# Start of a fused AdaLN, Mamba and mixture-of-experts kernel: order of the first loads, and products that keep TensorE occupied

## The chip, the cores and the metric

The kernel runs on one core of a Trainium2 chip. Its time is the device time of one execution in microseconds (us). An execution that the hardware profiler took is shown beside it; its span is counted from the first to the last instruction of the program. The engines are named as in the profile: PE is TensorE (matmuls; PEld are its weight loads), DVE is VectorE, ACT is ScalarE, POOL is GpSimd, and SP is SyncE, whose queue issues nearly all DMAs.

## The reference

There are 8 sequences of 2048 tokens with 256 features, all in fp32. A conditioning row per sequence gives six modulation vectors. The input is normalized and modulated, goes through a Mamba-2 mixer with a gated residual, is normalized and modulated again, and goes through a dense mixture of 8 experts with a second gated residual.

```python
mod = (_silu(c) @ wmod).reshape(8, 6, 1, -1)
sa, ca, ga, sb, cb, gb = (mod[:, n] for n in range(6))
ga, gb = ((2 * (g >= 0) - 1) * maximum(abs(g), 0.25) for g in (ga, gb))
h = _layernorm(x) * (1 + ca) + sa
# mixer: h @ W_in gives z, xBC, dt; a causal depthwise convolution of 4 taps and silu on xBC;
# a scan over chunks with decay exp(cumsum(dt * A)); times silu(z); RMS norm; @ W_out
x = x + ga * mixer(h)
h = _layernorm(x) * (1 + cb) + sb
# experts: softmax gate, weights under 0.1 set to zero, the rest normalized
x = x + gb * sum(weight[:, e] * (h @ expert_w[e] + expert_b[e]) for e in range(8))
```

## The kernel before

The tokens are cut into 32 blocks of 512 (4 blocks a sequence), and each block into 4 chunks of 128 for the scan. Each block passes through stages: `fetch` (its rows, `xt`), `first_norm`, `project_xbc` with the convolution behind it, `project_z`, `silu_xbc`, `spread` and `within` for each chunk, `outputs`, `output` with `residual`, `gate_weights`, `experts`. A stage is a generator. `at(time, stage)` puts it into a heap of planned times, `run()` resumes the stage that is due first, and `yield d` lets it sleep for d planned microseconds. Blocks start 70 planned us apart, and so several are in work at once. The plan is only made when the program is written down, and the framework's scheduler can still move instructions: what the chip sees is one fixed order on each engine, which waits in order for its operands by semaphores. PSUM's 8 banks are handed out by `take` and `give`; a bank counts as free `READ_TIME` after it was given back.

These are the parts at the start, with their lines in the profile of before:

- Loads before the stages: on SP's queue the first half of `wmod` (into `ht1`, line L109, in the profile `ht<-in_L_wmod_dram`), the rows of block 0 (`load(0, 0)`, L105), the part of `w_in` for `xbc`, `dt` and the rest (L109), convolution weights (L143, L144), the part for `z`, the small vectors (`d_ch` L152, `dt_bias` and `a_log` L148), `norm_sb` (L156), `wo_n` (L157), two pieces `wgate` and the second half of `wmod` (L109), and gate weights. ACT's queue loads the conditioning (L114), and ACT takes its silu (L115).
- `condition`: two transposes of the conditioning on PE (L252), copies to `ct` by DVE (L253), then `modulation(0)`: 8 products of 8 columns (L262; an fp32 product is two instructions in the trace) and two reads by DVE into `mod_pp` (L267).
- `first_norm` and `modulated`: statistics by DVE (L315, L316), `rstd` by POOL (L310, L311), `shift` by DVE (L324), `xn` by ACT (L328), transposes by PE (L338), and `ht` by ACT, which reads `mod_pp` (L340).
- `project_xbc`: 6 pairs of products (L409). Each bank is read by ACT (L364, and `halo` L368) and by three convolution taps on DVE (L372). `steps_of_time` stands beside it: `dt` products (L459), a softplus by Exp (L475) and Ln (L479) on ACT with steps on DVE between them (`sp_u` L481), and the running sum `cs` (L487). SP writes `cs` to DRAM (`cs_d`, L492), and `spread` reads it back to all partitions (`wide`, L512, 0.5 MB a chunk).
- `head_weights`: POOL copies `w_dt` (L177), and ACT takes the exponential of `a_log` (L178), for which it loads a table. `output_weights`: POOL scales `wo_n` (L276). `batch_gates`: products with `wgate` (L288).
- `expert_weights`: 4 loads of `eb_sb` (L168) and 8 of `we_sb` (L170), 0.25 MB each. In the order on SP's queue `cs_d` of block 0 stands behind the first `we_sb`, then come four more, `wide` of chunk 0, the last three, the rows of block 1, `wide` of chunk 1, and the rows of blocks 2 to 4.
- `within`: `w` and `wide` on ACT (L527, L541, L542), `xdt`, `sm` and `bm` on DVE (L545, L549, L551), `xdec` and `cw` on POOL (L558, L565), transposes and products on PE (L537 to L540, L576).

Of the kernel before, what the change touches and what calls it, by code (L numbers as in the profile page):

```python
# [15 lines left out]
P = 128  # L16
# [9 lines left out]
def kernel(  # L26
# [26 lines left out]
    nc = tc.nc  # L53
    B, L, DM = x.shape
# [10 lines left out]
    NC = T // P  # L65
    NSB = L // T
# [6 lines left out]
    def new(pool, shape, tag, bufs=None):  # L73
        n_names[0] += 1
        kw = {} if bufs is None else {"bufs": bufs}
        return pool.tile(shape, F32, tag=tag, name=f"{tag}_{n_names[0]}", **kw)
# [9 lines left out]
    upper = new(const, [P, P], "upper")  # L86
    make_upper_triangular(nc, upper, val=1.0, diag=True)
    ones = new(const, [P, P], "ones")
# [4 lines left out]
    io = ctx.enter_context(tc.tile_pool(name="io", bufs=5))  # L93
# [4 lines left out]
    sml = ctx.enter_context(tc.tile_pool(name="small", bufs=2))  # L98
    dram = ctx.enter_context(tc.tile_pool(name="dram", bufs=2, space=bass.MemoryType.DRAM))

    def load(b, s):
        xt = new(io, [P, NC, DM], "xt")
        nc.sync.dma_start(out=xt, in_=x[b, ts(s, T), :].rearrange("(c p) d -> p c d", p=P))  # L105
        return xt

    def columns(dst, src, first, count):
        nc.sync.dma_start(  # L109
            out=dst, in_=src[:, first : first + count].rearrange("(k p) n -> p k n", p=P)  # L110
        )
# [24 lines left out]
    nc.gpsimd.memset(w_dt, 0.0)  # L136
    a_pos = new(const, [P, 1], "a_pos")

    columns(wpp[0], wmod, 0, 2 * DM)
    first_x = load(0, 0)  # L140
    columns(w_in_sb[:, :, DI:], w_in, DI, NPROJ - DI)
    with nc.allow_non_contiguous_dma(reason="small vectors, an element or a few per partition"):
        nc.sync.dma_start(out=conv_w_sb, in_=conv_w.rearrange("(m p) k -> p m k", p=P))  # L143
        nc.sync.dma_start(out=conv_b_sb, in_=conv_b.rearrange("(m p) -> p m", p=P))  # L144
        columns(w_in_sb[:, :, :DI], w_in, 0, DI)
        for name, v in (("dt_bias", dt_bias), ("a_log", a_log)):
            for c in range(NC):
                nc.sync.dma_start(  # L148
                    out=heads[name][c * QD : c * QD + NH, :], in_=v.unsqueeze(1)
                )  # L150
        for q in range(2):
            nc.sync.dma_start(  # L152
                out=d_ch[ts(q, HEADDIM), :],
                in_=d_skip.rearrange("(m q) -> q m", q=2)[q].partition_broadcast(HEADDIM),
            )
        nc.sync.dma_start(out=norm_sb, in_=norm_w.rearrange("(m p) -> p m", p=P))  # L156
        nc.sync.dma_start(out=wo_n, in_=w_out.rearrange("(m p) o -> p m o", p=P))  # L157
        for g, part in enumerate((2, 5)):
            columns(wgate[:, :, g, :], wmod, part * DM, DM)
        columns(wpp[1], wmod, 3 * DM, 2 * DM)  # L160
        nc.sync.dma_start(
            out=gate_w_sb[:, :, :NE], in_=gate_w.rearrange("(k p) e -> p k e", p=P)
        )
    nc.sync.dma_start(out=heads["gate_b"], in_=gate_b.partition_broadcast(P))

    def expert_weights():
        for c in range(NC):
            nc.sync.dma_start(out=eb_sb[c * QD : c * QD + NE, c, :], in_=expert_b)  # L168
        for e in range(NE):
            nc.sync.dma_start(  # L170
                out=we_sb[:, :, e, :], in_=expert_w[e].rearrange("(k p) o -> p k o", p=P)
            )
            yield 2.0

    def head_weights():

        nc.gpsimd.tensor_copy(w_dt[:, :, :NH], w_in_sb[:, :, DI + CD : NPROJ])  # L177
        nc.scalar.activation(a_pos, heads["a_log"], AF.Exp)  # L178
        yield
# [6 lines left out]
    def at(time, stage):  # L186
        heapq.heappush(events, (time, n_events[0], stage))
        n_events[0] += 1
# [16 lines left out]
    def take(use, count=1):  # L205
        while True:
            now = clock[0]
            idle = sorted((t, i) for i, t in enumerate(free_at) if t <= now)
            held = sum(h == use and t > now for h, t in zip(holder, free_at))
            if len(idle) >= count and held + count <= MOST[use]:  # L210
                break
            yield 0.2
        got = []
        for _, i in idle[:count]:
            free_at[i], holder[i] = 1e9, use
            got.append(new(psum, [P, 512], f"bank{i}"))
            bank_of[got[-1].tensor.name] = i
        return got[0] if count == 1 else got

    def give(ps):  # L220
        free_at[bank_of.pop(ps.tensor.name)] = clock[0] + READ_TIME

# [2 lines left out]
        while any(step not in d for step in steps):  # L225
            yield 0.2

    order = [(b, s) for b in range(B) for s in range(NSB)]
    info = [{} for _ in order]
    gated, carry = {}, {}  # L230

# [7 lines left out]
        return t.unsqueeze(2).to_broadcast([P, NC, NE])  # L239

    def fetch(n):
        info[n]["x"] = first_x if n == 0 else load(*order[n])
        yield


# [1 line left out]
    ct = new(const, [P, KD, B], "ct")  # L247

    def condition():
        for k in range(KD):  # L250
            ps = yield from take("m")
            nc.tensor.transpose(ps[:, :B], cond_sb[:, ts(k, P)], ident[:B, :B])  # L252
            nc.vector.tensor_copy(ct[:, k, :], ps[:, :B])  # L253
            give(ps)
        yield from modulation(0)

    def modulation(half):
        ps = yield from take("m")
        for n in range(2):
            for d in range(KD):  # L260
                for k in range(KD):
                    nc.tensor.matmul(  # L262
                        ps[:, ts(n * KD + d, B)], wpp[half][:, k, n * DM + d * P :][:, :P],
                        ct[:, k, :], start=(k == 0), stop=(k == KD - 1),
                    )
        for n in range(2):
            nc.vector.tensor_scalar(  # L267
                mod_pp[:, 2 * half + n], ps[:, ts(n, KD * B)].rearrange("p (d b) -> p d b", b=B),
                float(n), None, ALU.add,
            )  # L270
        give(ps)

    def output_weights():

        for m in range(MI):
            nc.gpsimd.tensor_scalar(  # L276
                wo_n[:, m, :], wo_n[:, m, :], norm_sb[:, m : m + 1], None, ALU.mult
            )
        yield
# [475 lines left out]
    def experts(n):  # L755
# [32 lines left out]


    READ_TIME = 4.5  # L790
    PERIOD, XBC_STEP, Z_STEP, OUT_STEP = 70.0, 6.0, 3.5, 4.4
    STARTS = (
        (fetch, -20.0), (first_norm, -9.0), (project_xbc, 11.5), (project_z, 42.0),
        (silu_xbc, 47.5), (output, 128.0), (gate_weights, 156.0), (experts, 198.0),
    )
    at(-30.0, condition())
    at(12.0, head_weights())
    at(35.0, expert_weights())
    at(20.0, output_weights())
    at(30.0, modulation(1))  # L800
    for n in range(len(order)):
        start = n * PERIOD
# [41 lines left out]
```

## Time and profile before

| What | Before |
|---|---|
| median of 3 runs | 2406.21 us (2404.78 to 2408.36) |
| profiled execution, own time | 2408.26 us |
| its span | 2406.5 us |
| mean granted PE clock over the span | 0.988 |
| busy PE, DVE, ACT, POOL | 2327.3, 1830.3, 1621.4, 1128.7 us |
| HBM read, written | 89.47 MB, 18.87 MB |

The profile's page gives busy time by engine over the whole span. For the start, the answers by stretch give each engine's busy time, the granted PE clock and the DMA engines' share in a few microseconds, and the timeline gives every instruction with its start, its duration, and the idle time before it with what ended that. A wait counts only if the waiting engine, or one that waits for it, is late afterwards.

### The profile page before, as it was taken

The numbers are of one execution on the slowest core, as the hardware profiler recorded it, in microseconds if no ns is written. First come the engines' busy times: TensorE is split into PE (matmuls) and PEld (weight loads), VectorE is DVE, ScalarE is ACT, GpSimd is POOL, SyncE is SP. The second block draws the span as 40 slices with busy tenths as digits, with TensorE's granted clock in tenths as the row PEclk, the third lists the DMA queues.
The fourth block names the chain that finished last, engine by engine and source line by source line (L and its number), as shares of the span: only waits on it lengthen the run. The fifth ranks groups of instructions, "written<-read, shape, count | busy, mean of one in ns | idle before, by whom it ended". The sixth has DMA issues, their size and how long they took to land.

```text
span 2406.5 us, 33568 instructions
## 1 busy us (share of the span) xinstructions
PE 2327.3 (97%) x11602; PEld 1313.9 (55%) x11602; DVE 1830.3 (76%) x4414; ACT 1621.4 (67%) x2947; POOL 1128.7 (47%) x1244
## 2 busy tenths in 40 slices
PE   6889999999999999999999999999999999999998
PEld 3545555555555555555555555555555555555564
DVE  4777877777777787777887778777777787778775
ACT  6877676676666766667867667767677667667720
POOL 2554454443554435545445545445545445545442
PEclk8999999999999999999999999999999999999999
DMA  5111011110111101111111111111111111111100
GB/s 164 45 37 39 34 55 45 44 46 28 54 46 44 45 28 54 46 45 54 37 37 54 46 46 53 37 37 55 54 36 54 37 37 54 46 44 45 37 18 18
DMA packets 64601, 110.51 MB, mean 46 GB/s; under 512 B 7048, under 2 KB 47024, under 8 KB 64432
## 3 DMA queue, kind: packets, MB, share of 16 engines
q1 hardware_dynamic: 64416, 108.35, 13.3%
q8 instruction: 93, 1.52, 0.3%
q14 instruction: 76, 0.62, 0.1%
q10 hardware_dynamic: 16, 0.01, 0.0%
HBM read 89.47 MB, written 18.87 MB: 45 GB/s over the span
## 4 chain that ended last, share of the span: by engine, by line
PE 61%; ACT 11%; DVE 7%; POOL 6%; issue 1%; POOLq 0%; ACTq 0%
PE bank L781 26%; PE bank L662 8%; PE bank L409 7%; PE bank L445 6%; PE bank L608 4%; PE bank L576 3%; ACT w L527 3%; DVE xbc L372 2%; POOL cw L565 2%; PE bank L338 1%; PE bank L537 1%; ACT xn L328 1%; POOL rstd L311 1%; ACT wide L541 1%; DVE res L738 1%
## 5 line engine op out<-in xcount | busy, mean ns | idle before, releaser
L781 PE MATMUL bank<-we_sb,ht 128*128 128x512 f32 x2048 | 968.7, 598 | 18.3 <-DVE bm L551 15.6
L738 DVE SCALAR_TENSOR_TENSOR res<-bank,wt,res 128x256 f32<-128x256 f32 x1024 | 487.3, 476 | 212.6 <-PE bank L781 116.5
L781 PEld LDWEIGHTS bank<-we_sb,ht 128*128 128x128 f32 x2048 | 375.5, 191 | 398.8 <-issue 351.8
L372 DVE SCALAR_TENSOR_TENSOR xbc<-bank,conv_w_sb,xbc 128x511 f32<-128x511 f32 (+2 forms) x576 | 425.4, 740 | 96.0 <-ACT halo L368 94.9
L565 POOL TENSOR_TENSOR cw<-wide,xbc 128x1024 f32<-128x1024 f32 x128 | 305.7, 2388 | 274.5 <-ACT wide L541 157.2
L527 ACT ACTIVATE w<-wide,tok_major 128x128 f32<-128x128 f32 x1024 | 327.2, 390 | 137.8 <-PE bank L608 96.2
L409 PE MATMUL bank<-ht,w_in_sb 128*128 128x512 f32 x768 | 375.1, 611 | 5.6 <-DVE xbc L372 4.5
L445 PE MATMUL bank<-ht,w_in_sb 128*128 128x512 f32 x512 | 244.6, 601 | 1.0 <-ACT zs L432 1.0
L662 PE MATMUL bank<-wo,zs 128*128 128x256 f32 x1024 | 244.0, 380 | 0.3
L579 POOL TENSOR_TENSOR state<-state,wide 128x512 f32<-128x512 f32 x112 | 120.8, 1079 | 247.1 <-DVE state L590 216.7
L409 PEld LDWEIGHTS bank<-ht,w_in_sb 128*128 128x128 f32 x768 | 141.9, 194 | 163.6 <-issue 142.1
L340 ACT ACTIVATE ht<-bank,mod_pp 128x512 f32<-128x512 f32 x128 | 97.7, 776 | 188.9 <-PE bank L338 188.8
L364 ACT ACTIVATE xbc<-bank,conv_b_sb,conv_w_sb 128x512 f32<-128x512 f32 x192 | 147.3, 767 | 113.9 <-PE bank L409 113.0
L662 PEld LDWEIGHTS bank<-wo,zs 128*128 128x128 f32 x1024 | 189.9, 191 | 51.2 <-issue 26.4
L746 POOL TENSOR_TENSOR res<-res,gates 128x256 f32<-128x256 f32 x128 | 133.4, 1042 | 149.2 <-DVE res L738 142.4
L558 POOL TENSOR_TENSOR xdec<-xdt,tok_major 128x512 f32<-128x512 f32 x120 | 139.0, 1159 | 132.7 <-DVE xdt L545 130.5
L328 ACT ACTIVATE xn<-xt,shift,rstd 128x256 f32<-128x256 f32 x256 | 137.1, 591 | 89.2 <-DVE shift L324 89.2
L620 DVE SCALAR_TENSOR_TENSOR bank<-xbc,d_ch,bank 128x128 f32<-128x128 f32 x512 | 176.6, 349 | 20.7 <-PE bank L608 11.8
L562 DVE TENSOR_TENSOR w<-w,sm 128x1024 f32<-128x1024 f32 x128 | 189.0, 1477 | 0.0
L633 POOL TENSOR_TENSOR sq<-sq 128x256 f32<-128x256 f32 x128 | 99.2, 775 | 124.4 <-ACT sq L631 124.2
L445 PEld LDWEIGHTS bank<-ht,w_in_sb 128*128 128x128 f32 x512 | 91.0, 191 | 97.6 <-issue 90.6
L576 PE MATMUL bank<-xdec,bm 128*128 128x512 f32 x240 | 130.1, 625 | 12.7 <-POOL xdec L558 6.4
(129 smaller groups left out, 3364.6 us busy)
## 6 DMA issues: line engine op xcount, KB each, us to landing
wide<-cs_d SPq DMA_DIRECT2D x128, 512.0 KB
xt<-_attn_hidden_states_dram SPq DMA_DIRECT2D x32, 512.0 KB
out_dram<-xt SPq DMA_DIRECT2D x32, 512.0 KB
we_sb<-in_L_ffn_expert_w_dram SPq DMA_DIRECT2D x8, 256.0 KB
cs_d<-cs SPq DMA_DIRECT2D x32, 64.0 KB
ht<-in_L_wmod_dram SPq DMA_DIRECT2D x2, 512.0 KB
w_in_sb<-in_L_attn_W_in_dram SPq DMA_DIRECT2D x1, 776.0 KB
w_in_sb<-in_L_attn_W_in_dram SPq DMA_DIRECT2D x1, 512.0 KB
```

Of the source, the lines that this page charges most:

```text
L328: nc.scalar.activation(xn[:, c, :], src[:, c, :], AF.Identity, bias=shift[:, c : c + 1], scale=rstd[:, c : c + 1],)
L372: nc.vector.scalar_tensor_tensor(acc[:, ahead:], ps[:, : T - ahead], conv_w_sb[:, m, k : k + 1], acc[:, ahead:], ALU.mult, ALU.add,)
L409: nc.tensor.matmul(ps, w_in_sb[:, k, DI + m * P : DI + (m + 1) * P], ht[:, k, :], start=(k == 0), stop=(k == KD - 1),)
L445: nc.tensor.matmul(ps, w_in_sb[:, k, ts(m, P)], ht[:, k, :], start=(k == 0), stop=(k == KD - 1),)
L527: nc.scalar.activation(w[:, h, :], wide[:, h, :], AF.Relu, bias=tok_major[:, 1, c, h : h + 1])
L562: nc.vector.tensor_tensor(w, w, sm[:, None, :].to_broadcast([P, NH, P]), ALU.mult)
L565: nc.gpsimd.tensor_tensor(cw, wide, ct_[:, None, :].to_broadcast([P, NH, P]), ALU.mult)
L576: nc.tensor.matmul(st_ps[:, :DI], bm, xdec, start=True, stop=True)
L620: nc.vector.scalar_tensor_tensor(y[:, m, :], xbc[:, m, tok], d_ch[:, m : m + 1], y[:, m, :], ALU.mult, ALU.add,)
L662: nc.tensor.matmul(o_ps[:, :DM], d["zs"][:, m, ts(c, P)], wo[:, m, :], start=(m == 0), stop=(m == MI - 1),)
L738: nc.vector.scalar_tensor_tensor(res, ps[:, ts(q, DM)], wt[:, c, e + q : e + q + 1], res, ALU.mult, ALU.add)
L781: nc.tensor.matmul(ps, ht[:, k, ts(c, P)], we_sb[:, k, e : e + per, :].rearrange("p e o -> p (e o)"), start=(k == 0), stop=(k == KD - 1),)
```

## The change

Seven edits, all at the start. The rows of block 0 are loaded first, in four DMAs of 128 rows, ahead of the first half of `wmod`. The rows of block 1 are loaded ahead of `norm_sb`, `wo_n` and what follows, and no longer at the turn of their `fetch`. ACT copies `ct`. `modulation` waits a planned time between its products and its reads, 30 in the first half and 1 in the second. A new stage `warm` takes a bank and puts 15 products of two constant 128x128 tiles on PE, whose result nothing reads. `expert_weights` starts at planned time 60 in place of 35. The list `order` is made earlier, which changes nothing else.

```diff
+    first_x = new(io, [P, NC, DM], "xt")
+    for c in range(NC):
+        nc.sync.dma_start(out=first_x[:, c, :], in_=x[0, ts(c, P), :])
     columns(wpp[0], wmod, 0, 2 * DM)
-    first_x = load(0, 0)
     columns(w_in_sb[:, :, DI:], w_in, DI, NPROJ - DI)
...
+        second_x = load(*order[1])
         nc.sync.dma_start(out=norm_sb, in_=norm_w.rearrange("(m p) -> p m", p=P))
...
-        info[n]["x"] = first_x if n == 0 else load(*order[n])
+        info[n]["x"] = (first_x, second_x)[n] if n < 2 else load(*order[n])
...
-            nc.vector.tensor_copy(ct[:, k, :], ps[:, :B])
+            nc.scalar.copy(ct[:, k, :], ps[:, :B])
             give(ps)
-        yield from modulation(0)
-
-    def modulation(half):
+        yield from modulation(0, 30.0)
+
+    def warm():
+        ps = yield from take("m")
+        yield 40.9
+        for _ in range(WARM):
+            nc.tensor.matmul(ps[:, :P], ones, upper, start=True, stop=True)
+        give(ps)
+
+    def modulation(half, later=1.0):
...
+        yield later
         for n in range(2):
             nc.vector.tensor_scalar(
...
+    WARM = 15
...
     at(-30.0, condition())
+    at(-30.0, warm())
     at(12.0, head_weights())
-    at(35.0, expert_weights())
+    at(60.0, expert_weights())
```

In the changed program's written order one of the 15 products stands ahead of the modulation products, three behind them, one among the transposes of block 0, and ten between those and the first of L409. On ACT the table and exponential of `a_log` stand ahead of the first convolution step, and `Ln` ahead of the second. On SP `cs_d` stands behind two of the four `eb_sb`; two `eb_sb`, one `we_sb`, both first `wide`, seven `we_sb` and the rows of blocks 2 to 4 follow.

More of the change, by code (lines that the diff above doesn't have):

```diff
@@ L99 @@
     dram = ctx.enter_context(tc.tile_pool(name="dram", bufs=2, space=bass.MemoryType.DRAM))
+    order = [(b, s) for b in range(B) for s in range(NSB)]
     def load(b, s):
@@ L226, in until @@
             yield 0.2
-    order = [(b, s) for b in range(B) for s in range(NSB)]
     info = [{} for _ in order]
```

## Prediction

> **What bounds the kernel now.** I read the page's engine shares first, then busy time by stretch, then the order of time where TensorE (PE) is not full.
>
> ```profile
> PE 2327.3 (97%) x11602; PEld 1313.9 (55%) x11602; DVE 1830.3 (76%) x4414; ACT 1621.4 (67%) x2947; POOL 1128.7 (47%) x1244
> ...
> PEclk8999999999999999999999999999999999999999
> ```
>
> PE is busy 97% of the span; 79 us are left. Where they lie, the stretches say (engine busy and instruction counts, then granted PE clock, DMA share, GB/s):
>
> ```profile
> 0.00:10.00 10.00, 2.36 (x12) 2.30 (x12) 2.25 (x11) 1.70 (x2) 4.09 (x20) 1.00 0.84 239
> 10.00:20.00 10.00, 8.30 (x36) 4.39 (x35) 0.32 (x3) 4.27 (x7) 1.62 (x2) 1.00 0.54 153
> 20.00:30.00 10.00, 9.71 (x41) 5.15 (x35) 7.08 (x18) 7.04 (x15) 2.02 (x3) 1.00 0.13 39
> ...
> 40.00:50.00 10.00, 3.33 (x13) 1.85 (x11) 6.60 (x17) 9.72 (x11) 4.81 (x5) 0.75 0.69 235
> 50.00:60.00 10.00, 5.59 (x14) 2.61 (x15) 4.60 (x13) 4.41 (x12) 2.67 (x4) 0.50 0.16 52
> ...
> 1000.00:2300.00 1300.00, 1285.16 (x6481) 727.95 (x6480) 1013.34 (x2462) 904.79 (x1647) 633.12 (x685) 1.00 0.13 45
> ```
>
> Of the 79 us some 21 are in the first 60; from 1000 to 2300 PE idles 15 in 1300. So the bulk is PE work at full clock, which the change leaves alone, and only the start can gain. The start in order of time (start, duration; a bracket gives idle time before it and what ended it):
>
> ```profile
> 7.98 3.58 PE L262 MATMUL bank<-ct,ht 128*128 128x8 f32 x16 [3.90 <-DVE ct L253]
> 11.61 0.26 DVE L267 TENSOR_SCALAR mod_pp<-bank 128x16 f32<-128x16 f32 x2 [3.28 <-PE bank L262]
> 11.96 2.07 ACT L328 ACTIVATE xn<-xt,shift,rstd 128x256 f32<-128x256 f32 x4 [8.37 <-DVE shift L324]
> 15.44 3.78 PE L409 MATMUL bank<-ht,w_in_sb 128*128 128x512 f32 x4 [0.66 <-ACT ht L340]
> 25.10 0.29 DVE L481 SCALAR_TENSOR_TENSOR sp_u<-sp_u,sp_e 128x128 f32<-128x128 f32 x1 [1.94 <-ACT sp_l L479]
> 28.97 0.36 SPq L492 DMA_DIRECT2D cs_d<-cs  x1
> 43.34 0.43 DVE L315 BATCH_NORM_STATS2 stats<-xt 128x6 f32<-128x256 f32 x1 [2.53 <-DMA xt<-_attn_hidden_states_dram]
> 45.89 0.72 DVE L315 BATCH_NORM_STATS2 stats<-xt 128x6 f32<-128x256 f32 x2
> 48.15 2.29 DVE L324 SCALAR_TENSOR_TENSOR shift<-mv,rstd 128x4 f32<-128x4 f32 x1 [0.87 <-POOL rstd L311]
> 52.05 2.05 PE L576 MATMUL bank<-xdec,bm 128*128 128x512 f32 x2 [4.90 <-DVE bm L551]
> ```
>
> The reader is to see a chain: conditioning copy, modulation, block 0's normalization, its first projection (0.93 us a matmul where later ones step by 0.43), `cs` on VectorE (DVE), the `cs_d` DMA, and behind it on SyncE's (SP's) queue all expert weights and block 1's rows. DVE waits 2.53 us for these, then comes block 2's first statistic (second of the pair at 45.89), the `shift`, and only then `bm`, for which PE waits.
>
> **The change part by part.** The changed program's order on each engine differs from before only up to block 1's first half; behind that every engine has the same order. So a gain at about 50 us is carried to the end, and nothing multiplies.
>
> Conditioning copy and modulation. ACT copies `ct`: two small copies of 0.15 (the `halo` copies' time) while ACT idles from 3.6 to 11.96; nothing queues behind but `xn`. DVE's copies stood behind block 0's statistics, which waited for `xt` until 6.04, so modulation began at 7.98. It now waits for `wmod` alone, which has moved behind the rows: four issues of some 0.5 in place of one put it about 1.5 later on SP. The same 1.05 MB stand ahead of it as ahead of the statistics at 6.04; with the slower issue I take 6.4 (6.0 to 7.0). The read of `mod_pp` still stands before `shift` in DVE's order, in spite of its later time in the plan, so that part moves nothing: zero. Modulation ends at 10.0, `xn` begins at 10.4: 1.6 earlier.
>
> Unused products. 15 fp32 products are 30 instructions of 128 columns, a quarter of L409's: 0.22 cold (0.93/4), 0.11 warm. One is hidden in idle time before modulation, three (1.3) and one (0.4) hold the transposes a little, which then end near 13.3 (before 14.78). Ten (20 instructions) stand ahead of L409, whose `ht` would be ready about 14: cold they cost 4.4 and L409 begins at 17.7, 2.3 later than before; what they can buy is the clock. The clock column has no record before 21.06 and prints 1.00; the steps of 0.93 and then 0.43 show a half clock until about 21. Later a row tells what brings it back:
>
> ```profile
> 58.60:62.02 3.42, 3.42 (x16) 1.81 (x14) 0.00 (x0) 0.12 (x1) 0.00 (x0) 0.50 0.00 0
> 62.02:65.40 3.38, 3.31 (x22) 1.58 (x22) 2.12 (x5) 3.35 (x4) 0.28 (x1) 1.00 0.00 0
> ```
>
> One full stretch of 3.4 us, here half of it L338's transposes, and the clock is whole. In the changed order PE is full from 10.0 on, so the first whole window of 3.4 ends between 13.4 and 16.8; I take 15.0. By then 8 of the 20 are done; 12 warm ones take 1.3, L409 begins at 16.3 and its four take 1.7: 18.0 against 19.2 before. [...] The row has eight transposes in the very window that raised the clock, so I take 18.0 and keep 19.8 (20.5 at worst) for the range.
>
> To `cs`. ACT now loads the table for `a_pos` before the first convolution step, and runs `Ln` right behind `Exp` and ahead of the second step. Before, `sp_u` started at 25.10, 5.9 after L409's first four. Now: `halo` 0.9 after them, `Exp` by 1.25, table 1.28, `Ln` 0.31: 2.9 after. From there to the `cs_d` issue it is 3.9 as before (25.10 to 28.97). So `cs_d` goes at 18.0+2.9+3.9 = 24.8, 4.1 earlier; by the rule of transposes at 26.6.
>
> Loads. Block 1's rows move past `norm_sb`, `wo_n`, both `wgate` and the second `wmod` half on SP; each lands up to 1.5 later (0.5 MB at 350 GB/s). POOL's L276 waits for `wo_n` at 18.38 and then has nothing until 34.6; PE reads the others at 27.3 and 30, and in the changed order at about 25 and 27, when they are there since about 22.5. Without that cover it would be 1.5. Rows of block 1 are there by 16, so the 2.53 wait goes. What is late next is block 2's rows, whose statistic stands on DVE between block 1's fourth and its sum. Before they landed at about 46.1 (the pair at 45.89 did not wait; DMA share falls from 1.02 to 0.31 after 46), 17.1 after `cs_d`. Bytes behind `cs_d` up to them were 3.9 MB, and are 3.7 (block 1's 0.52 gone, one 0.26 expert more): 1.0 less at before's rate, but two of the small expert-bias loads now stand between: 16.4 after `cs_d`, so 41.2. Without any wait DVE would be there at 40.1 (46.25 less the 2.53 and less 3.6, since PE's last convolution product now follows `cs`, modulation and gates, 5.3 of work, and gives back 0.5 of the 4.1), so DVE waits about 1 us. That is 4.9 earlier than 46.1. `wide` twice in succession moves the second one forward; ACT reads it at 52.5, where nothing waited. Experts loaded later are first read at 156: zero.
>
> From there on the train is as before: POOL's `rstd`, its `cw` of 2.34 starting with DVE's `shift`, which then takes 2.29 in place of 0.15 (ACT's silu ahead of `cw` is done before `rstd`, as before, so this stays), `bm`, L576. Sum: span 2406.5 - 4.9 = 2401.6. That execution's own time was 2408.3, 2.1 above the median of the three runs, so it becomes 2403.4, and against the median 2406.2 - 4.9 = 2401.3.
>
> **The rivals.** (1) The wait for block 2 takes more of the gain: products hold L409 to 19.8, or the loads behind two adjoining `wide` are slower, so that 17.5 is the delay. Each leaves 3 to 4 us: 2402.5 to 2403.5, no difference. For it: DMA ran at 210 to 275 GB/s just behind `cs_d`. Against it: fewer bytes. That the products do not bring the clock is its other form, 2404.5 at worst.
>
> (2) The start gains more: POOL's `cw` waits for ACT's silu, so `shift` escapes it (2.1 more), or the clock stays up: 2396 to 2399. Against it: DVE's wait for block 2 gives ACT time to finish.
>
> (3) Slower. The shifted start meets other clock windows while the pipeline fills (60 to 200 us), where PE has gaps of 1 to 3 us and lies at half clock around 76, 106, 130 and 164, some 17 us in all (granted clock 0.93 over 60 to 200 is 20 us at half, 2 of them at 60 to 62). Half clock costs half its length where PE is full. Against a gain of 4.9 it decides from 10 us more of half clock; with 7 us more in each of four blocks, 27, it costs 13.7: 2415. Against it: these runs lie within 3.6 us of one another.
>
> **How the numbers follow.** My forecast, with its larger variant (2), has 0.55: faster by over 0.2%, which is 4.8 us and about what a measurement of this kernel can tell from no change. It sits at that edge; rival (1) has 0.35, rival (3) 0.10. The likeliest case's own range is 2397 to 2402; down to 2395.5 takes in (2), up to 2407 takes in (1) with the costs at their dear ends.
>
> **What would show it.** Right: modulation at 6 to 7, L409's matmuls at 0.43 from the first, its four done by 18, `cs_d` at about 25, no wait for rows of block 1, DVE waiting about 1 us for rows of block 2, and L576 at about 47. Wrong: L409 in steps of 0.93; `cs_d` later than 27; block 2's rows at 44 or later; more half clock between 60 and 200 than 17 us.

## The result, and the profile after

The changed kernel's median is 2401.72 us (2398.83 to 2404.67, 22 runs), against 2406.57 us (2400.43 to 2408.66, 22 runs) for the kernel before on the same chip: 4.85 us less, a ratio of 0.9982 with a 95% interval of 0.9975 to 0.9988. The profiled execution took 2401.53 us with a span of 2399.7; that of before took 2408.26 with 2406.5. So the profiles differ by 6.8 us of span and the medians by 4.85, because the profiled execution of before lay 1.7 above its median. Lines of the changed kernel are the old ones plus 13 or 14: L262 is now L275, L328 L342, L409 L423, L492 L506, L315 L329, L324 L338, L576 L590, and `cw` (L565) L579. In the experiments the numbers move by a few lines more; the names of the tiles tell which operation it is.

The engine shares and the clock by slice, from the page of the changed kernel:

```profile
PE 2325.9 (97%) x11632; PEld 1316.3 (55%) x11632; DVE 1829.1 (76%) x4412; ACT 1621.5 (68%) x2949; POOL 1127.9 (47%) x1244
...
PEclk9999999999999999999999999999999999999999
```

There are 30 PE instructions more, the 15 products, and the first slice of the clock is a 9 where it was an 8. The stretches (busy time of PE, PEld, DVE, ACT, POOL, then granted clock, DMA share, GB/s):

```profile
0.00:10.00 10.00, 3.86 (x18) 3.60 (x18) 2.27 (x9) 1.97 (x4) 4.07 (x20) 1.00 0.83 232
10.00:20.00 10.00, 10.00 (x63) 7.95 (x64) 1.28 (x6) 6.12 (x11) 0.00 (x0) 1.00 0.21 59
20.00:30.00 10.00, 9.77 (x36) 5.16 (x36) 8.55 (x20) 8.68 (x15) 3.70 (x4) 1.00 0.75 245
...
40.00:50.00 10.00, 2.86 (x8) 1.12 (x8) 6.63 (x21) 9.90 (x13) 5.80 (x6) 0.75 0.43 138
50.00:60.00 10.00, 8.95 (x42) 4.69 (x42) 2.90 (x7) 6.60 (x13) 1.13 (x1) 0.74 0.00 0
1000.00:2300.00 1300.00, 1285.30 (x6472) 727.71 (x6472) 1011.65 (x2450) 903.16 (x1647) 632.43 (x685) 1.00 0.13 45
```

From 1000 to 2300 nothing has changed: PE idles 15 in 1300 as before. The gain is a start that is over sooner: between 50 and 60 PE is busy 8.95 where it was 5.59. The steps of that start, in order of time:

```profile
7.21 3.55 PE L275 MATMUL bank<-ct,ht 128*128 128x8 f32 x16 [2.95 <-DMA ht<-in_L_wmod_dram]
11.16 2.07 ACT L342 ACTIVATE xn<-xt,shift,rstd 128x256 f32<-128x256 f32 x4 [7.43 <-DVE shift L338]
16.48 1.88 PE L423 MATMUL bank<-ht,w_in_sb 128*128 128x512 f32 x4
21.34 0.31 ACT L493 ACTIVATE sp_l<-sp_u 128x128 f32<-128x128 f32 x1
25.56 0.36 SPq L506 DMA_DIRECT2D cs_d<-cs  x1
36.82 0.42 DVE L329 BATCH_NORM_STATS2 stats<-xt 128x6 f32<-128x256 f32 x1
40.59 0.90 DVE L329 BATCH_NORM_STATS2 stats<-xt 128x6 f32<-128x256 f32 x2
43.02 0.16 DVE L338 SCALAR_TENSOR_TENSOR shift<-mv,rstd 128x4 f32<-128x4 f32 x1 [0.87 <-POOL rstd L325]
43.78 2.36 POOL L579 TENSOR_TENSOR cw<-wide,xbc 128x1024 f32<-128x1024 f32 x1 [0.80 <-ACT xbc L441]
44.98 1.98 PE L590 MATMUL bank<-xdec,bm 128*128 128x512 f32 x2 [0.34 <-DVE bm L565]
```

The reader is to see this: the modulation waits for `wmod` and is 0.77 earlier; the four L423 step by 0.43 but begin a microsecond later (16.48 against 15.44); `cs_d` goes 3.41 earlier; block 1's statistics (36.82) wait for nothing; the pair with block 2's first one takes 0.90 in place of 0.72, so that wait is some 0.2; `shift` takes 0.16, because here `cw` waited 0.80 for ACT's silu and began after it; and L590 is 7.07 earlier than before's 52.05. From block 1's first L423 on, the distance to the end stays as it was: that product is at 56.48 (before 62.73), 6.25 earlier, and from it to the end of the span are 2343.2 (before 2343.8).

### The profile page after: what moved, and what is told of

Same layout as the page of the kernel before. It is cut to its first block, busy times and chain, and to the rows that moved or that the text cites. A ratio compares the mean times of both kernels' runs of the same rounds, so it can differ in the third digit from the quotient of the medians.

```text
span 2399.7 us, 33630 instructions
## 1 busy us (share of the span) xinstructions
PE 2325.9 (97%) x11632; PEld 1316.3 (55%) x11632; DVE 1829.1 (76%) x4412; ACT 1621.5 (68%) x2949; POOL 1127.9 (47%) x1244
## 3 DMA queue, kind: packets, MB, share of 16 engines
q1 hardware_dynamic: 64464, 108.35, 13.7%
## 4 chain that ended last, share of the span: by engine, by line
PE 62%; ACT 11%; DVE 7%; POOL 6%; issue 1%; POOLq 0%; ACTq 0%; DVEq 0%
PE bank L795 26%; PE bank L676 8%; PE bank L423 7%; PE bank L459 6%; PE bank L622 4%; PE bank L590 3%; ACT w L541 3%; DVE xbc L386 2%; POOL cw L579 2%; PE bank L352 1%; PE bank L551 1%; ACT xn L342 1%; POOL rstd L325 1%; ACT wide L555 1%; DVE res L752 1%
## 5 line engine op out<-in xcount | busy, mean ns | idle before, releaser
L795 PE MATMUL bank<-we_sb,ht 128*128 128x512 f32 x2048 | 968.8, 598 | 17.9 <-DVE bm L565 15.5
L579 POOL TENSOR_TENSOR cw<-wide,xbc 128x1024 f32<-128x1024 f32 x128 | 306.6, 2396 | 276.1 <-ACT wide L555 157.9
L423 PE MATMUL bank<-ht,w_in_sb 128*128 128x512 f32 x768 | 371.2, 606 | 5.1 <-DVE xbc L386 4.5
L593 POOL TENSOR_TENSOR state<-state,wide 128x512 f32<-128x512 f32 x112 | 120.8, 1078 | 247.6 <-DVE state L604 220.1
L423 PEld LDWEIGHTS bank<-ht,w_in_sb 128*128 128x128 f32 x768 | 140.5, 192 | 160.9 <-issue 140.8
L676 PEld LDWEIGHTS bank<-wo,zs 128*128 128x128 f32 x1024 | 189.6, 191 | 51.1 <-issue 26.8
L342 ACT ACTIVATE xn<-xt,shift,rstd 128x256 f32<-128x256 f32 x256 | 137.1, 591 | 87.8 <-DVE shift L338 87.8
L576 DVE TENSOR_TENSOR w<-w,sm 128x1024 f32<-128x1024 f32 x128 | 189.4, 1480 | 0.0
L622 PEld LDWEIGHTS bank<-w,xdt 128*64 128x64 f32 x2048 | 112.9, 137 | 50.8 <-issue 19.3
```

The source lines that it names most:

```text
L342: nc.scalar.activation(xn[:, c, :], src[:, c, :], AF.Identity, bias=shift[:, c : c + 1], scale=rstd[:, c : c + 1],)
L423: nc.tensor.matmul(ps, w_in_sb[:, k, DI + m * P : DI + (m + 1) * P], ht[:, k, :], start=(k == 0), stop=(k == KD - 1),)
L576: nc.vector.tensor_tensor(w, w, sm[:, None, :].to_broadcast([P, NH, P]), ALU.mult)
L579: nc.gpsimd.tensor_tensor(cw, wide, ct_[:, None, :].to_broadcast([P, NH, P]), ALU.mult)
L622: nc.tensor.matmul(y_ps[ts(q, HEADDIM), ts(m, P)], lhs[:, ts(h, HEADDIM)], rhs[:, h, :], start=(i == 0 and m == 0), stop=(i == len(parts) ...
L676: nc.tensor.matmul(o_ps[:, :DM], d["zs"][:, m, ts(c, P)], wo[:, m, :], start=(m == 0), stop=(m == MI - 1),)
```

## The experiments

All were timed in five rounds against the kernel before. Ratios are against the runs of before beside them; intervals are some 0.0013 to 0.002 wide, so a difference between two kernels of some 2 us is at the edge of what they tell apart, in direction and not in size, and one of 1 us is not told apart. In each, the framework writes the orders anew, and what moved with the edit is said.

**Without the unused products.**

```diff
-    at(-30.0, warm())
```

> The changed kernel without its 15 unused products. In the written order ACT's table for a_pos and Ln then stand where they stood before the change (behind the first and second convolution step). Theory A (a chain to cs_d, whose shift is carried to the end, and the products pay by clock and by ACT's order): L409 begins about 14.9, a matmul each 0.93, its four end about 18.5, cs_d goes near 28 in place of 25.6, and the time is 2 to 3 us above the changed kernel: about 2404.3 against 2406.5 before. Theory B (the gain is in the loads alone, the ten products ahead of L409 only delay it): L409's four end 1 to 2 earlier than 18.4, cs_d before 25, the time 1 to 2 us below the changed kernel: about 2400.3.

Measured: 2402.48 us, ratio 0.9988 (0.9980 to 0.9996). By the ratios that is 1.4 us above the changed kernel (0.9982), by the medians 0.8: the direction of the first theory, but not clear of the noise. The order on ACT turned back with it: `a_pos` and `Ln` stand behind convolution steps again. DVE's order moved too: block 2's first statistic stands behind block 1's sums. Two stretches, and rows of its timeline, show what the clock did (its first record in this profile is at 18.04, and before that the column prints 1.00):

```profile
11.21:14.62 3.41, 2.17 (x8) 1.15 (x8) 0.01 (x1) 2.79 (x6) 0.00 (x0) 1.00 0.02 0
14.62:18.04 3.42, 3.31 (x4) 1.17 (x4) 0.00 (x0) 0.73 (x2) 0.00 (x0) 1.00 0.04 0
```

```profile
14.73 3.61 PE L423 MATMUL bank<-ht,w_in_sb 128*128 128x512 f32 x4 [0.65 <-ACT ht L354]
27.40 0.34 SPq L506 DMA_DIRECT2D cs_d<-cs  x1
```

The four L423 are cold, some 0.9 each, but they begin 1.75 earlier than with 15 products, and end at 18.34, where the changed kernel ends them at 18.37. So in these two profiles the 15 products bring the clock and use up what it brings. What is later here is `cs_d` (27.40): `Ln` begins 4.67 after the four, in place of 2.97. DVE then waits 2.99 for block 2's rows, to 45.30, and L590 begins at 48.12 behind them and a `shift` of 0.67.

**Eight products in place of 15.**

```diff
-    WARM = 15
+    WARM = 8
```

> The changed kernel with 8 unused products in place of 15; three in place of ten stand right ahead of L409, and ACT's table and Ln stand as before the change. Theory A: L409 begins about 15.5, its four end at 17.5 to 18.5 because the clock is still brought by products and transposes, cs_d near 26.5 to 27, since Ln is late again: 1 us above the changed kernel, about 2402.7. Theory B: half of the products, half of their delay: about 2401, cs_d about 25.

Measured: 2402.69 us, ratio 0.9985 (0.9978 to 0.9991): what the first theory had, and not told apart from the changed kernel. The four L423 run from 14.68 and end at 16.66, the earliest of all, and yet `cs_d` goes at 25.77: ACT's order has `Ln` behind the second step, and it begins 4.67 after the four. Up to `cs_d`, an earlier clock and a later `Ln` cancel.

**Loads at their old places.**

```diff
-        second_x = load(*order[1])
-        info[n]["x"] = (first_x, second_x)[n] if n < 2 else load(*order[n])
+        info[n]["x"] = first_x if n == 0 else load(*order[n])
-    at(60.0, expert_weights())
+    at(35.0, expert_weights())
```

> The changed kernel with block 1's rows and the expert weights in their old places on SP's queue (block 0's rows stay first, in four pieces). Theory A: cs_d still goes near 25.6; block 1's rows land 14.3 behind it as before, near 40, DVE waits for them about 3 us, block 2's rows land near 42.7, L576 is 1.5 to 2 us later than the changed kernel's 44.98, and the time is about 2403.5. Theory B (the loads are all of the gain): the whole gain goes, 2406.5.

Measured: 2402.96 us, ratio 0.9989 (0.9980 to 0.9997), near the first theory, with an interval that overlaps that of the changed kernel. Block 1's statistics wait for rows again, 0.42, and block 2's 0.53. POOL's order changed too: `cw` stands behind the second `rstd`, and so it is block 2's `shift` that takes 2.30, and L589 begins at 51.44 behind it.

**Block 0's rows in one transfer behind `wmod`.**

```diff
-    first_x = new(io, [P, NC, DM], "xt")
-    for c in range(NC):
-        nc.sync.dma_start(out=first_x[:, c, :], in_=x[0, ts(c, P), :])
     columns(wpp[0], wmod, 0, 2 * DM)
+    first_x = load(0, 0)
```

> The changed kernel with block 0's rows in one DMA behind the first half of wmod, as before the change. Theory A: wmod lands at 4.5 and modulation, whose ct comes from ACT, runs 4.6 to 8.2; statistics begin at 6.0, shift at 9.6, xn at 9.8 in place of 11.2, L409's four end about 17.5 in place of 18.4: about 1 us below the changed kernel, 2400.9. Theory C (rows first are what starts the chain earlier): xn at 11.8 or later, 1.5 us above the changed kernel, 2403.2.

Measured: 2404.61 us, ratio 0.9994 (0.9985 to 1.0002). Every theory missed it. The modulation begins at 4.65 and `xn` at 9.67, 1.5 earlier than in the changed kernel, and nothing comes of it. DVE does two of block 1's statistics, at 19.59 and 21.46, in the middle of the steps to `cs`, so `Ln` begins 4.6 after the four L421, and further down POOL has `cw` behind the second `rstd`:

```profile
46.10 2.35 POOL L577 TENSOR_TENSOR cw<-wide,xbc 128x1024 f32<-128x1024 f32 x1
46.16 2.30 DVE L336 SCALAR_TENSOR_TENSOR shift<-mv,rstd 128x4 f32<-128x4 f32 x1 [1.41 <-POOL rstd L323]
49.01 2.04 PE L588 MATMUL bank<-xdec,bm 128*128 128x512 f32 x2 [4.27 <-DVE bm L563]
```

`shift` begins 0.06 after `cw` and ends with it; `bm` stands behind it, and L588 is 4 us later than in the changed kernel. This line is in before's profile too, at 48.15. Of these four runs each has it in another form: block 2's `shift` takes 2.30 in two of them, block 1's 0.67 in the run without products, and with 8 products no `shift` is long. So the next runs take it out.

**`shift` of blocks 1 and 2 by POOL.** The same edit in three kernels: before, the changed kernel, and the one with block 0's rows behind `wmod`. All orders are otherwise those of the kernel edited.

```diff
-        nc.vector.scalar_tensor_tensor(shift, mv[:, :, 0], -1.0, rstd, ALU.mult, ALU.mult)
+        if half == 0 and any(keep is info[n] for n in (1, 2)):
+            nc.gpsimd.tensor_tensor(shift, mv[:, :, 0], rstd, ALU.mult)
+            nc.gpsimd.tensor_scalar(shift, shift, -1.0, None, ALU.mult)
+        else:
+            nc.vector.scalar_tensor_tensor(shift, mv[:, :, 0], -1.0, rstd, ALU.mult, ALU.mult)
```

> The kernel before, with the `shift` of blocks 1 and 2 (first norm) written by GpSimd as a product and a negation instead of by one VectorE operation; all orders are otherwise those of before. In before VectorE's `shift` of block 1 took 2.29 us because GpSimd's cw was running (0.16 alone), and the bm product, L576 and the next block's rows came behind it. Theory A (the part of the change's gain beyond the earlier start came from that collision falling away): block 1's shift comes some 0.3 us after rstd on GpSimd's own queue and VectorE goes from its last statistics straight on to bm, L576 begins about 2 us earlier than before's 52.05, so about 50, and the time is 1.8 to 2.1 us below before (ratio 0.9992). Theory B (the collision was covered, the path to L576 went by the projection and its products): L576 moves by under 0.5 and the time is that of before within 0.5.

Measured: 2403.09 us, ratio 0.9986 (0.9977 to 0.9995): 3.1 us less than before, which is the first theory; its 1.8 to 2.1 lie inside the interval (1.2 to 5.5). Its timeline:

```profile
46.17 0.20 POOL L325 TENSOR_TENSOR shift<-mv,rstd 128x4 f32<-128x4 f32 x1
46.44 0.28 DVE L555 COPY bm<-bank 128x128 f32<-128x128 f32 x1
46.66 2.35 POOL L569 TENSOR_TENSOR cw<-wide,xbc 128x1024 f32<-128x1024 f32 x1
46.86 2.04 PE L580 MATMUL bank<-xdec,bm 128*128 128x512 f32 x2 [0.39 <-DVE bm L555]
```

`cw` is as long as ever, but DVE is at `bm` before it starts. L580 comes 5.2 earlier than L576 in before, of which some 2 belong to rows that landed earlier in this execution (block 1's first statistic, which had waited for its rows to 43.34 in before, ran at 41.26).

> The changed kernel with the same edit (block 1's and block 2's first-norm `shift` by GpSimd). In the changed kernel's profile block 1's shift took 0.16 us on VectorE and only block 2's took 1.00. Theory A (the collision had already fallen away): nothing left to gain at block 1, L576 within 0.5 of 44.98, the time within 0.5 us of the changed kernel, 0.9982 of before. Theory B (in the changed kernel the collision is still there in the other executions and the profiled one was a lucky one): 1 to 2 us below the changed kernel, 0.9975 of before.

Measured: 2399.34 us, ratio 0.9975 (0.9965 to 0.9985): 2.4 us less than the changed kernel by the medians, 1.7 by the ratios: the second theory. The nine runs lie between 2397.66 and 2400.85, where 14 of the changed kernel's 22 lie above 2400.85. This version has the lowest median of all; its interval overlaps that of the changed kernel. That the free `shift` in the changed kernel's profile was not its usual case would explain the gain, but it is not shown. The edit also takes block 2's `shift`, which took 1.00 in that profile and stood ahead of the copy of `state` (48.46; here 47.59), and block 1's first L427 is at 55.52 here against 56.48 there, without any collision at block 1 in either. So up to 1 us of the gain can be block 2's.

> The changed kernel with block 0's rows again in one transfer after wmod, and the `shift` of blocks 1 and 2 by GpSimd. With the rows in one transfer and the shift on VectorE xn came 1.5 us earlier than in the changed kernel but the run took 2404.6, with block 2's shift taking 2.30 us beside cw and bm behind it. Theory A (that collision took the gain): the time falls by 2 to 3 us against that run, to about 2402, 0.9983 of before. Theory B (the loss lies elsewhere, in block 2's rows that arrive 1.9 us late or in cw itself being late on GpSimd's queue): L576 stays near 49 and the time at 2404 to 2405.

Measured: 2402.24 us, ratio 0.9989 (0.9980 to 0.9998): 2.4 less than with `shift` on DVE by the medians, as the first theory had it, and 1.2 by the ratios, which is not clear of the noise. It stays 2.9 behind the run with `shift` on POOL and four early pieces, measured beside it, and here there is no overlap: the lowest of its 11 runs, 2401.30, lies above the highest of the other nine, 2400.85. So the four pieces ahead of `wmod` are the part of the change whose worth is plainest, though their absence lets the modulation begin earlier (5.10 against 6.83). In the profile `Ln` begins 4.6 after the four L425 and `cs_d` goes at 27.48 (26.24), DVE waits 2.76 for block 2's rows, to 44.66, and L592 begins at 47.68 (45.50). As the orders on DVE and POOL changed with the loads, the share of each is open.

**`ct` copied by DVE again.**

```diff
-            nc.scalar.copy(ct[:, k, :], ps[:, :B])
+            nc.vector.tensor_copy(ct[:, k, :], ps[:, :B])
```

> The changed kernel with the conditioning's columns copied out of PSUM by VectorE again instead of ScalarE. Theory A (the modulation waits for wmod's landing at 7.2, and the columns are there by 6 either way): the time is that of the changed kernel, 0.9982 of before, and the modulation still begins at wmod's landing. Theory B (VectorE's copy, behind statistics of block 0, makes the columns the last to come): the modulation begins 0.5 to 1 us later and the time is 0.5 to 1 us above the changed kernel.

Measured: 2401.50 us, ratio 0.9983 (0.9974 to 0.9991), the changed kernel's time. With rows ahead of `wmod`, DVE is past block 0's statistics in time, and this part of the change is worth nothing that shows. All other orders are those of the changed kernel, so its profile is nearly a second one of the changed kernel, and there block 1's `shift` collides:

```profile
42.83 0.43 DVE L329 BATCH_NORM_STATS2 stats<-xt 128x6 f32<-128x256 f32 x1 [1.11 <-DMA xt<-_attn_hidden_states_dram]
43.39 1.06 ACT L441 ACTIVATE xbc<-xbc 128x1024 f32<-128x1024 f32 x1
43.71 1.04 POOL L325 TENSOR_TENSOR rstd<-rstd,neg_half 128x4 f32<-128x4 f32 x1
44.73 2.35 POOL L579 TENSOR_TENSOR cw<-wide,xbc 128x1024 f32<-128x1024 f32 x1
44.79 2.31 DVE L338 SCALAR_TENSOR_TENSOR shift<-mv,rstd 128x4 f32<-128x4 f32 x1 [0.87 <-POOL rstd L325]
48.72 2.04 PE L590 MATMUL bank<-xdec,bm 128*128 128x512 f32 x2 [2.67 <-DVE bm L565]
```

Here block 2's rows come 16.0 after `cs_d` (26.81) and DVE waits 1.11 for them. So `rstd` is done at 44.75, after ACT's silu (44.45); `cw` starts at once, and `shift` 0.06 behind it. In the changed kernel's own profile the rows came earlier, `rstd` was done at 42.98 and the silu only at 43.71. Which of the two is last decides over 2 us at L590. It need not show in the time of one execution: this one, with the collision, took 2399.94, less than the changed kernel's 2401.53 without it, because what follows block 1's first L423 (58.92 here) was 2339.2 long, 4.0 shorter (last section).

**The products and the loads, judged with `shift` on POOL.** Both start from the kernel with 2399.34. POOL's order is the same without the products, while ACT's and DVE's change as in the run without them above; without the early loads `cw` moves behind the second `rstd`.

```diff
-    at(-30.0, warm())
```

> The changed kernel with block 1's and block 2's first-norm `shift` by GpSimd, and without the 15 unused products; GpSimd's order is the same with and without them. So the chance meeting of shift and cw is out of the comparison, and the products are judged alone against the run with shift by GpSimd (2399.3). Theory A (the products bring the full clock early and with it `cs_d`, which sets the rest): L423's first four in steps of about 0.9, `cs_d` 1.5 to 2 us later than with them, L590 as much later, the time 2400.8 to 2401.3. Theory B (what the products gain at `cs_d` is taken back by ScalarE's work and block 2's rows): `cs_d` later by as much, but L590 by under 0.5, and the time within 0.5 of 2399.3.

Measured: 2401.84 us, ratio 0.9984 (0.9975 to 0.9993): 2.5 us more than with the products by the medians and 2.2 by the ratios, the first theory in direction and just beyond its upper end in size. The four run from 14.15 to 17.93, `Ln` begins 4.77 after them, `cs_d` goes at 26.93, L594 at 46.00, and block 1's first L427 at 56.76 (with products 26.24, 45.50 and 55.52, in one profile each). The two intervals overlap; the run with the fill below, which has the products and was timed beside this one, took 2400.21, 1.6 us less. So the products are worth 1.6 to 2.5 us here, near the limit of the noise.

```diff
-        second_x = load(*order[1])
-        info[n]["x"] = (first_x, second_x)[n] if n < 2 else load(*order[n])
+        info[n]["x"] = first_x if n == 0 else load(*order[n])
-    at(60.0, expert_weights())
+    at(35.0, expert_weights())
```

> The changed kernel with shift by GpSimd as above, but with block 1's rows and the experts back at their old places on SyncE's queue. Theory A (block 2's rows come later with 0.5 MB more behind `cs_d`, and the projection's last product first when block 1's rows are late): block 1's statistics wait again, 0.4 to 2.5 us, L590 1 to 2.5 us later than with shift by GpSimd alone, the time 2400.3 to 2401.8. Theory B (ScalarE's silu, not the rows, sets L590 once the shift is out of the way): within 0.5 of 2399.3.

Measured: 2401.93 us, ratio 0.9981 (0.9973 to 0.9990): 2.6 us more by the medians, 1.4 by the ratios. The time is that of the first theory, its mechanism is not in the profile: block 1's statistics did not wait, and L593 was 0.55 later. The second L593, at 51.66, waited 1.67 for `xdec`, which stood behind this `cw`:

```profile
47.17 1.23 DVE L579 TENSOR_TENSOR w<-w,sm 128x1024 f32<-128x1024 f32 x1 [0.87 <-ACT w L559]
47.18 3.43 POOL L582 TENSOR_TENSOR cw<-wide,xbc 128x1024 f32<-128x1024 f32 x1
```

So the kernel is slower without the early loads, at the limit of the noise, but what this profile shows as the cause is POOL's order, which their absence changed. That the earlier rows themselves gain is not shown.

**More products in PE's next idle stretch.**

```diff
+        if (n, c) == (0, 1):
+            for _ in range(FILL):
+                nc.tensor.matmul(b_ps[:, :P], ones, upper, start=True, stop=True)
         nc.tensor.transpose(b_ps[:, :P], bt, ident)
...
+    FILL = 16
```

> The changed kernel with shift by GpSimd, and 16 more unused products, about 3.5 us of TensorE, in its wait for ScalarE's silu of block 0 at 40 to 44; every other order is unchanged. In all profiles so far the granted clock fell to a half at 42 to 45 behind this idle stretch, for 10 to 17 us. Theory A (the idle stretch brings the half clock, and the half clock costs at L590, 2.05 us for two, which VectorE's state copy and w wait for): full clock until about 47 or later, the two L590 in about 1.1, block 1's first L423 1 to 2 us earlier, the time 2397.3 to 2398.3. Theory B (ScalarE, busy without a gap from 38 to 52, sets the pace there and TensorE's clock does not matter): the clock stays up, but block 1's first L423 and the time stay within 0.5.

Measured: 2400.21 us, ratio 0.9975 (0.9965 to 0.9985), the same ratio as without them: the second theory. One stretch of `shift` by POOL alone, and of the same with the fill:

```profile
44.00:48.00 4.00, 3.52 (x8) 1.68 (x8) 1.51 (x6) 3.96 (x4) 3.74 (x5) 0.50 0.07 10
```

```profile
44.00:48.00 4.00, 2.08 (x9) 0.99 (x8) 2.63 (x9) 3.96 (x4) 3.66 (x6) 1.00 0.01 4
```

The two pairs of L597, from the timeline with the fill:

```profile
45.70 1.10 PE L597 MATMUL bank<-xdec,bm 128*128 128x512 f32 x2 [0.34 <-DVE bm L572]
51.22 2.08 PE L597 MATMUL bank<-xdec,bm 128*128 128x512 f32 x2 [1.85 <-POOL xdec L579]
```

The clock stays whole to 50.68 and is half for 3.4 us there, in place of 10.2 from 43.45 on; the first pair takes 1.10 in place of 2.05, and the next pair waits for POOL's `xdec` all the same. ACT is busy 3.96 of 4.00 in both, and block 1's first L427 comes at 55.90 (without the fill 55.52). The half clock of 10 to 17 us behind 44, the most striking thing in this part of the profile, costs nothing that shows here.

**ACT's order without the products.** Without products, and with the first two convolution steps of block 0 made to wait for `a_pos` and `Ln`:

```diff
+    def later_bias(m, src):
+        t = new(const, [P, 1], f"bias{m}")
+        nc.scalar.activation(t, src, AF.Identity, bias=conv_b_sb[:, m : m + 1], scale=0.0)
+        info[0]["bias", m] = t
...
-    at(-30.0, warm())
```

> The changed kernel with shift of blocks 1 and 2 by GpSimd and without the 15 products, as in the run without products (2401.8), but with ScalarE's order at the start held as the changed kernel has it: the table and exponential of `a_log` ahead of the first convolution step, `Ln` ahead of the second. It is held by data: the first two steps of block 0 take their bias from a copy that ScalarE makes behind those operations (two operations of one column more). In all profiles `Ln` begins 2.9 to 3.0 us after L423's first four where the order is this one, and 4.7 to 4.8 us after where the second step stands ahead; the first four themselves end at 18.4 to 19.6 with the products and at 17.9 to 18.3 without. Theory A (the products gain by the order that the planner makes of them, not by the clock): `Ln` 2.0 to 3.0 us after the first four, `cs_d` at 25 to 25.5, L590 at 44.5 to 45.5, and the time 2398.5 to 2400, that of the changed kernel with shift by GpSimd. Theory B (the early clock is what gains): `cs_d` is earlier, but the time stays at 2401.3 to 2402.3.

Measured: 2402.74 us, ratio 0.9985 (0.9975 to 0.9994). It settles nothing. `Ln` was not brought to where the expectation needed it: the first step fell between Exp and the table that `Ln` needs, so `Ln` came 4.26 after the four and `cs_d` at 26.74; DVE's order changed as well. That the products gain through ACT's order and not through the clock is what the rows of the runs above say; it is argued, not shown.

## Why the prediction was right, and where its steps were not

The total, 2401.3, is 0.4 from the median. The steps behind it did less well, and that it came so close is in part luck: errors of both signs stand behind it. The frame held: the gain lies in the start, and it is carried to the end.

- **Modulation at 6.4, `xn` at 10.4.** Mis-sized. `wmod` landed at 7.21, and in nine more profiles with the same loads ahead of it the modulation began between 6.65 and 8.11. The 1.5 for four issues was right in kind and too small (`wmod` was issued at 2.61, in before at 0.72). It hardly mattered: a modulation 2.6 earlier, and `xn` 1.5 earlier, with `wmod` first gave nothing.
- **Full clock at 15.0, four L423 done at 18.0.** In this profile 14.34 and 18.37; in three others with the same start (`shift` on POOL, that with the fill, `ct` on DVE) the first record of full clock is at 16.1 to 16.6 and the four end at 19.0 to 19.6, near rival (1)'s 19.8. Here the clock came behind a full stretch of 3.41 us, as argued, but against before's 19.22 the four gained 0.85 at best. The term that failed is the price of the ten products ahead of L423: without any, the four end at 17.9 to 18.3. No run shows what the prediction's 19.8 (20.5 at worst) for the four and its 26.6 for `cs_d` rest on; in these four profiles the four were done at 18.37 to 19.6, and `cs_d` went at 25.56 to 26.8.
- **Transposes and the clock.** The second of these two stretches of the changed kernel ends where the full clock is first recorded:

```profile
7.50:10.93 3.43, 3.43 (x17) 3.43 (x17) 0.13 (x2) 0.00 (x0) 0.20 (x1) 1.00 0.90 217
10.93:14.34 3.41, 3.41 (x17) 3.27 (x17) 0.20 (x3) 2.21 (x5) 0.00 (x0) 1.00 0.02 0
```

  The second is full, and all eight transposes begin in it (from 12.03), 2.09 us in all. The unused products in it come to 2.12 at most, and in before a stretch of the same length with 2.20 of L409 did not raise the clock (its first record is 21.06):

```profile
14.23:17.64 3.41, 2.75 (x6) 1.32 (x6) 0.00 (x0) 1.45 (x2) 0.00 (x0) 1.00 0.82 199
```

  So the stretch that raised the clock was full only with its transposes, as the prediction's row was. The first stretch, full of modulation products of 8 columns, did not raise it: the six unused instructions from 10.61 on still take 1.63, 0.27 each, where the last twenty, from 14.17 on, take 2.48, 0.12 each. Busy is not enough, and what else it takes no run here shows.
- **`Ln` 2.9 after the four, `cs_d` 3.9 after `sp_u`.** Right: 2.97 and 3.88 (21.68 to 25.56). `cs_d` was to go at 24.8 and went at 25.56, in three other profiles at 26.2 to 26.8: the two terms above.
- **Loads.** Block 1's wait is gone. `wo_n` landed late (POOL had it at 23.80) and was covered until 36. The second `wmod` half was not there at 22.5: PE waited 0.23 for it at 26.46.
- **Block 2's rows 16.4 after `cs_d`, DVE waiting about 1 us.** 16.0 and 1.11 with `ct` on DVE; some 15.4 and 0.2 in the changed kernel's profile, 15.7 and 0.80 with `shift` on POOL. The step was right.
- **"so this stays".** This is the step that failed in the profiled execution: `shift` escaped, which was rival (2). The reason is in ACT's train. It was to come 3.6 earlier with everything else, and its silu came only 1.85 earlier (44.50 to 42.65), since ACT waited 1.92 for PE's last convolution product at 31.99. The prediction's argument against rival (2), that DVE's wait for block 2 gives ACT time, is just what the profile with `ct` on DVE shows. The run with `shift` on POOL, where some 2 us were left to gain, suggests that this case is a common one; how common, the records don't show.
- **Sum.** L590 was to be at about 47, 4.9 earlier. It was at 44.98 (7.07 earlier) where `shift` was free and at 48.72 (3.33 earlier) where it was not; the median's 4.85 lies between. The share of each is not known, and L590 is not the whole path: block 1's first L423 was 6.25 and 3.81 earlier in the same two profiles.
- **Rival (3).** The half clock between 60 and 200 did not grow with the shifted start: some 14 us, where before had 17 beyond 62. And in the run with the fill most of the half clock behind 44 went, and no gain showed.

## What to carry to other kernels

When a part of the chain sits in the start of a pipelined kernel, cost it by the event that ends last there, and look for two engines' operations that begin within a tenth of a microsecond of each other: which one is first can be worth more than the edit (here a `shift` of 0.16 or of 2.3 us). An edit in a kernel whose orders are planned also re-makes the orders, so compare these first, and test an effect again with the accidental one taken out: the products and the loads made a difference near the limit of the noise only after `shift` had left DVE, and even then the orders had moved with them. A long stretch at half clock is no cost until something that waits for it is found late: with 3.4 us of it in place of 10.2 behind 43, no gain showed here.

## What the runs showed of the hardware

DVE's `shift` on 128x4 elements takes 0.16 us, and 2.29 to 2.31 when it starts 0.06 after POOL's `cw` of 2.35, ending with it; started in mid-`cw` it took 0.67 (45.65 to 46.32, `cw` to 46.30, in the run without products). It works the other way too: `cw` took 3.43 where DVE's `w` of 1.23 had begun 0.01 before it. In the run without the early loads that is 1.07 more than `cw`'s usual 2.36, of the 1.22 that `w` still had to run. In these rows the price is about the partner's remaining time, not the operation's own length: the long `shift` ends within 0.02 us of `cw` each time. Not every operation pays it: DVE's second `bm`, at 46.83 beside `cw` in before with `shift` on POOL, took 0.28 like the one begun ahead of it. What makes the two wait for one another, the rows don't show.

The spread of a kernel's times, some 8 us for before, goes with the mean granted clock of each run: of the 49 runs of before beside the first four experiments the 33 at 0.989 average 2406.4 us and the five at 0.991 average 2402.8. The profiles show where some of it lies. From block 1's first product with `w_in` (L423 or its like) to the end are 2342.3 to 2343.8 us in twelve of the fourteen profiles, in which the clock is at half for 20.5 us between 200 and 2300; in the other two (`ct` on DVE, and before with `shift` on POOL) it is at half for 13.7 us there, and the same distance is 2339.2 and 2340.1. Half of the 6.8 us between them, 3.4, is about what the distance is shorter by. That half clock lies between 560 and 1020, far behind what the edits change, so these 3 to 4 us come on top of what the start gains or loses, and one profile's total can hide it. What decides which of the two an execution gets, the records don't show.
